# Issuing a transformer kernel's second batch from ScalarE before the first attention unit, and moving that batch's norm

## The chip, the core and the metric

The kernel runs on one core of a Trainium2 chip, as one launch. The metric is the device time in microseconds of one execution, taken as the median of several. Five engines work on their own instruction streams, each in its own order: PE (TensorE, matmuls), ACT (ScalarE), DVE (VectorE), POOL (GpSimd) and SP (SyncE, which only issues DMAs here). ACT and POOL can issue DMAs as well; such an issue stands in their stream like any other instruction. In the profile SPq and ACTq are these issues, PEld is PE's loading of weights. All arithmetic is in 32-bit floats. "Round" and "unit" below are words of this kernel.

## What is computed

Two transformer layers over x of shape (4, 512, 320), with a context of shape (4, 1601, 192). Each layer is:

```
h1 = layernorm(x) * n1_g + n1_b
x  = softmax((h1 q1)(h1 k1)^T / 4) (h1 v1) o1_w + o1_b + x        # 20 heads of 16
h2 = layernorm(x) * n2_g + n2_b
x  = softmax((h2 q2)(ctx k2)^T / 4) (ctx v2) o2_w + o2_b + x      # 1601 keys
h3 = layernorm(x) * n3_g + n3_b
a, g = split(h3 ff_w1 + ff_b1)
x  = (a * gelu(g)) ff_w2 + ff_b2 + x
```

## The kernel before

The work is cut into units: for each layer, self attention (4 batches by 5 groups of 4 heads), cross attention (the same 20), and one feed-forward unit per batch. A self-attention unit has 4 key chunks of 128. For every unit the kernel computes, ahead of the unit itself,

- the projections (`both`, line 786): two calls per unit, `proj` in the chains below. PE multiplies the normalised tokens hT by q1 and k1 (line 794), ACT brings the result out as `low` (line 810; for the first unit ACT makes `high`, line 805, and DVE `low`, line 806), and POOL splits it into a high and a low part (`split`, lines 714 and 715; not for the first unit).
- the moves (line 762): six DMAs that bring high and low parts of keys and queries into the places from which PE reads them. In the opening they go to SP and ACT in turn, high parts by SP and low parts by ACT.
- the values (`values`, line 926 on PE, copied by ACT at line 933): two parts by four chunks of tokens per batch, of 128 and of 192 columns.
- the row maxima (`max_pairs`): rounds of 8 matmuls into 4 PSUM banks (line 992), each bank reduced by DVE (line 1007). A self-attention unit has four rounds. `max_end` (lines 1057 to 1069) turns the maxima into rows `nrows`, by one DVE transpose and four small DMAs, in the opening by SP, ACT, POOL and SP.

The unit itself (`main`, line 1189) computes scores (line 1199), takes the exponential on ACT (line 1209), multiplies by the values (line 1225), and adds up on POOL (line 1245), with rounds of maxima of the next unit between. A batch's norm (`add_norm`) has, in the chain `norm`: four steps of statistics on DVE (lines 520, 521); two steps that find 1/sqrt by Newton's method (three DVE operations at lines 484 to 488, then line 490 and three times lines 497 to 500, on DVE while `start["on"]` holds and on POOL afterwards); four steps that normalise (line 537, DVE); three that transpose on PE and bring hT out (ACT, line 560; in the opening the middle one on DVE, line 555), each followed on POOL by adding a bias row `brow` to x (line 566).

In the steady state chains of such tasks are picked by due time and a credit of PE time, round by round (`steps`, `pick`, `pace`). Ahead of the first unit the order is written out by hand: the lines that the diff removes at its end. PSUM has 8 banks, and `bank` gives each new tile the bank that a table of assumed costs (`written`, `busy`) expects to be free first. Every instruction waits in its engine's order until what it needs is there, so a tile given a bank whose old content has not been read yet holds PE up.

Loads before the change, all by SP, in this order: x of batch 0 in four pieces of 160 KB (line 160), the norm's scales and shifts lng and lnb (three small DMAs each, line 198), q1, k1 and v1 in three pieces each (line 193), two bias rows brow broadcast to 128 partitions (line 201), x of batch 1 in four pieces. After them come the six moves of the first unit.

Of the kernel before, what the change touches and what calls it, by code (L numbers as in the profile page):

```python
# [9 lines left out]
F32 = mybir.dt.float32  # L10
# [14 lines left out]
NQ = N // P  # L25
# [41 lines left out]
def kernel(ctx: ExitStack, tc: tile.TileContext, x, context, ws, out):  # L67
# [16 lines left out]


    nc = tc.nc
    dma = nc.sync.dma_start

    const = ctx.enter_context(tc.tile_pool(name="const", bufs=1))
    wpool = ctx.enter_context(tc.tile_pool(name="weights", bufs=1))  # L90
# [36 lines left out]
    room = {"turn": 0, "first": 0}  # L127
# [27 lines left out]
    def load_x(b):  # L155

        src = x[b].rearrange("(c p) d -> p c d", p=P)

        def part(t):
            dma(out=xs[b][:, t], in_=src[:, t])  # L160
            loaded[b] = clock["round"] if t == NQ - 1 else 1 << 30

        return [lambda t=t: part(t) for t in range(NQ)]
# [24 lines left out]
    def now(fs):  # L188
        for f in fs:
            f()  # L190
# [9 lines left out]
    def load_row(t, v):  # L200
        dma(out=t, in_=v.rearrange("(o d) -> o d", o=1).to_broadcast([P, D]))

    def load_bias(l, i):
        if i > 2:
            l, i = l + 1, i - 3
        if l < L:
            load_row(brow[(3 * l + i) % 2], ws[l][("o1_b", "o2_b", "ff_b2")[i]])
# [8 lines left out]
    def load_self(l):  # L216
        return [lambda: load_norm(l, 0)] + [
            f for t, n in ((wq1, "q1"), (wk1, "k1"), (wv1, "v1")) for f in load_rows(t, ws[l][n], DK)
        ]
# [107 lines left out]
    units = []  # L327
# [35 lines left out]
    stage = [0] * B  # L363


    start = {"on": True}

# [52 lines left out]
    def run(chain):  # L422
        costs, _, ready, _, f = chains[chain].popleft()
        assert ready(), chain
        f()
        clock["credit"] -= sum(costs)
# [54 lines left out]
    def guess_root(var):  # L481

        a, h, y, z = (two.tile([P, NQ], F32, tag=f"root{i}", name=f"root{i}") for i in range(4))
        nc.vector.tensor_scalar(a, var, EPS, None, ALU.add)
        nc.vector.tensor_scalar(
            z.bitcast(I32), a.bitcast(I32), 1, None, ALU.logical_shift_right
        )
        nc.vector.tensor_scalar(y.bitcast(I32), z.bitcast(I32), -1, 0x5F3759DF, ALU.mult, ALU.add)
        eng = nc.vector if start["on"] else nc.gpsimd
        eng.tensor_scalar(h, a, -0.5, None, ALU.mult)  # L490
        return h, y, z

    def better_root(h, y, z):


        eng = nc.vector if start["on"] else nc.gpsimd
        eng.tensor_tensor(z, y, y, ALU.mult)
        eng.tensor_tensor(z, z, h, ALU.mult)
        eng.tensor_scalar(z, z, 1.5, None, ALU.add)
        eng.tensor_tensor(y, y, z, ALU.mult)  # L500
# [216 lines left out]
    def add_proj(u):  # L717
        chain = "early" if u.early else "proj"
# [3 lines left out]
        first = units[u.i - u.g]  # L722
# [29 lines left out]
        def move(of, pairs, may, gap=0):  # L752

            def f():
                pending[of] -= 1
                u.moving[of] = clock["round"]
                for to, src in pairs():
                    queue = nc.sync
                    if start["on"]:
                        queue = (nc.sync, nc.scalar)[room["first"] % 2]  # L760
                        room["first"] += 1
                    queue.dma_start(out=to.bitcast(F32), in_=src)
                u.open -= 1
                if not u.open:
                    u.when = -9 if start["on"] else clock["round"]

            pending[of] += 1
            u.moves[of].append((f, may, gap))
            u.moving[of] = clock["round"]
            if (u.i, of, u) not in movers:  # L770
                movers.append((u.i, of, u))
# [273 lines left out]
    def max_reduce(u):  # L1045
        if u.pm is not None:
            nc.vector.tensor_reduce(
                u.nm.rearrange("p (j t) -> p t j", t=NQ), u.pm, AX.X, ALU.max, negate=True
            )
            busy("dve", 0.25)  # L1050

    def max_end(u):

        parts = two.tile([P, SLOT], F32, tag="parts", name="parts")
        high, low = (parts.rearrange("p (j e t) -> p e j t", e=2, t=NQ)[:, e] for e in range(2))
        of = u.nm.rearrange("p (j t) -> p j t", t=NQ)
        nc.vector.tensor_copy(high.bitcast(F32R), of)
        nc.vector.tensor_tensor(low, of, high, ALU.subtract)
        turned = two.tile([P, SLOT], F32, tag="turned", name="turned")

        nc.vector.transpose(turned, parts)
        busy("dve", 0.6)
        slots = u.rows.bitcast(F32).rearrange("(g s) n -> s g n", s=DH)[0].rearrange("g (t r) -> g t r", t=NQ)

        def rows():
            for i in range(P // SLOT):
                part = slice(i * SLOT, (i + 1) * SLOT)
                queue = (nc.sync, nc.scalar, nc.gpsimd, nc.sync)[i] if start["on"] else nc.sync
                queue.dma_start(out=slots[:, :, part], in_=turned[part, :])

        if u.cross and u.before.cross:
            errands.appendleft((clock["round"] + 1, yes, rows))
        else:
            rows()
# [368 lines left out]
    def at_once(v):  # L1443
        chain = "early" if v.early else "proj"
        while not v.keyed:
            if not chains[chain][0][2]():
                for w in attn:
                    for todo in w.moves.values():
                        while todo and todo[0][1]():
                            todo.popleft()[0]()  # L1450
            run(chain)
        for todo in v.moves.values():
            while todo:
                assert todo[0][1]()
                todo.popleft()[0]()
# [60 lines left out]

    take_rooms(0)
    now(load_x(0))
    now(load_self(0))
    load_bias(0, 0)  # L1520
    load_bias(0, 1)
    now(load_x(1))

    add_norms(0)
    add_proj(units[0])
    warm(5)
    until(lambda: not chains["proj"], "proj")
    at_once(units[0])
    add_proj(units[1])
    add_values(units[0])  # L1530
    run("proj")
    run("proj")
    for _ in range(2 * NQ + 2):
        run("norm")
    at_once(units[1])
    add_proj(units[2])
    first = units[0]
    first.pairs = max_pairs(first)
    for chain in ("proj", "proj", "values", None):
        round_of(first.pairs[0].popleft() + first.pairs[1].popleft())  # L1540
        if chain:
            run(chain)

    at_once(units[2])
    run("values")
    max_reduce(first)
    max_end(first)
    loads.extend(load_x(2))
    for fs in (load_out(0, "o1_w"), load_x(3), load_cross(0)):
        loads.extend(fs)  # L1550
    second = units[1]
    second.pairs = max_pairs(second)
    for _ in range(2):
        round_of(second.pairs[0].popleft() + second.pairs[1].popleft())
        run("values")
        run("values")
    start["on"] = False
    clock["credit"] = 0.0

# [46 lines left out]
```

## Time and profile before

| | |
|---|---|
| median of 3 runs | 3083.38 us (3080.82 to 3083.61) |
| the profiled execution | 3081.84 us |
| its span, first to last instruction | 3080.1 us |
| TensorE clock granted, mean | 0.988 |
| busy: PE, DVE, ACT, POOL | 97%, 72%, 64%, 37% of the span |
| first matmul of the first unit's scores | 43.41 us into the span |

The times in the timeline are microseconds from the span's start: start, duration, engine, line, operation, what is written and read, how often, and in brackets how long the engine was idle before it and what ended that. Consecutive instructions of one kind are one row. DMA rows tell of the issue, not of the transfer. The view by stages gives for each stretch its length, then busy time and number of instructions of each engine, the granted clock, the busy share of the DMA engines and GB/s.

### The profile page before, as it was taken

To read this page: it belongs to the slowest core of one execution; us is meant where nothing else is said; L and a number is where in the kernel's file an instruction comes from. 1 tells how busy PE (TensorE), PEld (TensorE's weight loads), DVE (VectorE), ACT (ScalarE), POOL (GpSimd) and SP (SyncE) were. 2 spreads that over 40 slices of the span, in tenths; PEclk is the share of its full clock that TensorE was granted. 3 is DMA by queue.
4 is the path that set the end of the run, shared out by engine and by line. 5 is a ranking of instruction groups with operands and counts; after the bars stand their busy time and mean duration, and the time that the engine had idled before them with its cause. 6 is when DMAs were issued, how large, how long until landed. Compare 5 with 4: busy or idle time off the path is not lost.

```text
span 3080.1 us, 82562 instructions
## 1 busy us (share of the span) xinstructions
PE 2986.1 (97%) x34290; PEld 1615.6 (52%) x34290; DVE 2220.3 (72%) x4240; ACT 1962.2 (64%) x3909; POOL 1125.7 (37%) x1209
## 2 busy tenths in 40 slices
PE   8999999999999999999999999999999999999999
PEld 5555455555555555455555555555545555544555
DVE  6987888888888888422258888888888888784221
ACT  4776577877877878611137765778778778784110
POOL 3444234544544544301114442445444444431000
PEclk9999899999999999999999999999999999999999
DMA  4433222221221221300113331212121122102000
GB/s 104 127 85 98 53 63 57 62 59 35 62 59 34 62 54 27 83 6 0 31 45 106 84 81 51 61 50 47 43 55 42 43 59 47 44 16 80 9 13 13
DMA packets 188327, 165.62 MB, mean 54 GB/s; under 512 B 67748, under 2 KB 152880, under 8 KB 187952
## 3 DMA queue, kind: packets, MB, share of 16 engines
q1 hardware_dynamic: 187160, 159.15, 20.2%
q8 instruction: 270, 4.42, 0.6%
q10 hardware_dynamic: 760, 1.18, 0.1%
q14 instruction: 105, 0.86, 0.1%
q0 software_dynamic: 32, 0.00, 0.0%
HBM read 43.53 MB, written 28.90 MB: 24 GB/s over the span
## 4 chain that ended last, share of the span: by engine, by line
PE 75%; DVE 21%; ACT 1%; issue 1%; POOL 1%; SPq 1%; DMA 0%; ACTq 0%; DVEq 0%
PE av L1225 18%; PE st L1199 15%; DVE pm L1007 10%; PE fps L1328 9%; PE sps L992 8%; PE yps L1385 6%; DVE nmax L1007 4%; PE kps L860 3%; PE qkps L794 3%; PE ops L1127 3%; PE vps L945 3%; PE fps L1342 2%; PE vps L926 2%; PE qps L835 1%; PE sps L1019 1%; DVE oturn L1095 1%
## 5 line engine op out<-in xcount | busy, mean ns | idle before, releaser
L1209 ACT ACTIVATE pr<-st 128x512 f32<-128x512 f32 (+1 forms) x2720 | 1408.2, 604 | 318.1 <-PE st L1199 249.1
L1007 DVE TENSOR_REDUCE pm<-sps 128x1 f32<-128x512 f32 x1920 | 1183.7, 680 | 76.7 <-PE sps L992 67.5
L1245 POOL TENSOR_TENSOR o<-o,vo 128x512 f32<-128x512 f32 x576 | 739.5, 1284 | 1257.1 <-ACT vo L1244 1245.7
L992 PE MATMUL sps<-kT,q 32*128 32x512 f32 x4800 | 960.9, 443 | 29.7 <-DVE x L1134 11.3
L1199 PE MATMUL st<-q,kT 32*128 32x512 f32 (+1 forms) x5120 | 837.3, 427 | 8.8 <-DVE pm L1007 8.6
L1225 PE MATMUL av<-pr,vals 128*32 128x512 f32 (+1 forms) x5440 | 746.9, 614 | 33.3 <-DVE pm L1007 10.2
L1199 PEld LDWEIGHTS st<-q,kT 32*128 32x128 f32 (+1 forms) x5120 | 442.6, 181 | 409.9 <-ACT pr L1209 214.7
L1199 PE MATMUL st<-nrows,ones 32*128 32x512 f32 (+1 forms) x2720 | 565.2, 407 | 0.3 <-DMA nrows<-turned 0.3
L992 PEld LDWEIGHTS sps<-kT,q 32*128 32x128 f32 x4800 | 456.7, 186 | 137.8 <-DVE pm L1007 46.9
L1007 DVE TENSOR_REDUCE nmax<-sps 128x1 f32<-128x512 f32 x640 | 395.1, 681 | 74.7 <-PE sps L992 72.5
L1244 ACT COPY vo<-av 128x512 f32<-128x512 f32 x576 | 352.2, 612 | 51.3 <-PE av L1225 50.0
L1353 ACT ACTIVATE gl<-fps,b 128x512 f32<-128x512 f32 x80 | 54.7, 687 | 374.0 <-PE fps L1342 267.8
L1328 PE MATMUL fps<-hT,w 128*128 128x512 f32 x640 | 283.5, 596 | 0.0
L1225 PEld LDWEIGHTS av<-pr,vals 128*32 128x32 f32 (+1 forms) x5440 | 112.3, 108 | 296.8 <-DVE pm L1007 136.3
L1199 PEld LDWEIGHTS st<-nrows,ones 32*128 32x128 f32 (+1 forms) x2720 | 253.8, 181 | 17.3 <-issue 1.1
L1354 DVE SCALAR_TENSOR_TENSOR hid<-fps,b,gl 128x512 f32<-128x512 f32 x80 | 59.8, 750 | 238.6 <-ACT gl L1353 236.2
L1328 PEld LDWEIGHTS fps<-hT,w 128*128 128x128 f32 x640 | 119.4, 190 | 148.9 <-issue 146.7
L1385 PE MATMUL yps<-w,hid 128*128 128x320 f32 x640 | 175.7, 434 | 0.0
L1385 PEld LDWEIGHTS yps<-w,hid 128*128 128x128 f32 x640 | 120.7, 190 | 55.1 <-ACT gl L1353 4.5
L1127 PEld LDWEIGHTS ops<-wo,aT 112*32 112x32 f32 (+1 forms) x3072 | 97.2, 110 | 65.1 <-issue 43.8
L1127 PE MATMUL ops<-wo,aT 112*32 112x160 f32 (+1 forms) x3072 | 123.8, 300 | 3.9 <-DVE pm L1007 3.6
L1392 DVE TENSOR_TENSOR x<-yps,x 128x320 f32<-128x320 f32 x32 | 15.7, 492 | 153.4 <-PE yps L1385 153.4
(90 smaller groups left out, 2562.4 us busy)
## 6 DMA issues: line engine op xcount, KB each, us to landing
kT<-stages SPq DMA_DIRECT2D x160, 192.0 KB
oway<-o SPq DMA_DIRECT2D x80, 256.0 KB
q<-high SPq DMA_DIRECT2D x160, 64.0 KB
q<-low SPq DMA_DIRECT2D x160, 64.0 KB
kT<-high SPq DMA_DIRECT2D x60, 128.0 KB
q<-high SPq DMA_DIRECT2D x60, 128.0 KB
kT<-low SPq DMA_DIRECT2D x57, 128.0 KB
aT<-oway SPq DMA_DIRECT2D x32, 224.0 KB
```

Source lines behind the costliest of these rows:

```text
L794: nc.tensor.matmul(ps[:, :w], lhsT=wqk[:n, k, u.g].rearrange("p i d -> p (i d)"), rhs=first.hT[:n, k, at : at + w], start=(k == 0), stop=( ...
L860: nc.tensor.matmul(ps[i * GD : (i + 1) * GD, :w], lhsT=wk_q[rows, k, u.g * GD : (u.g + 1) * GD], rhs=first.kvT[rows, k, i * HALF : i * HAL ...
L992: nc.tensor.matmul(ps, lhsT=u.q[j * SLOT : (j + 1) * SLOT, e, t * P : (t + 1) * P], rhs=u.kT[j * SLOT : (j + 1) * SLOT, u.k0 + s * 512 : u ...
L1007: nc.vector.tensor_reduce(to[:, j : j + 1], ps, AX.X, ALU.max, negate=(ns == 1))
L1127: nc.tensor.matmul(ps[f : f + m, : D // 2], lhsT=aT[:n, k, t * P + f : t * P + f + m], rhs=wo[:n, k, cols], start=(k == 0), stop=(k == 2),)
L1199: nc.tensor.matmul(st[:r, :], lhsT=ones[rows, :r] if e == 2 else u.keys(rows, c), rhs=u.rows[rows, :] if e == 2 else u.q[rows, e, :], star ...
L1209: nc.scalar.activation(p[:r], st[:r], AF.Exp)
L1225: nc.tensor.matmul(ps[j * SLOT : (j + 1) * SLOT, :], lhsT=columns_of[:r, head : head + SLOT], rhs=pr.pop((c, j))[:r, :], start=True, stop= ...
L1244: nc.scalar.copy(vo, ps)
L1245: nc.gpsimd.tensor_tensor(u.o, u.o, vo, ALU.add)
L1328: nc.tensor.matmul(ps, lhsT=w1[:, k, i * FF + c * P : i * FF + (c + 1) * P], rhs=u.hT[:, k, :], start=ahead and k == 0, stop=not ahead and ...
L1385: nc.tensor.matmul(ps[:, :D], lhsT=hid[c][:, t * P : (t + 1) * P], rhs=w2[:, c, :], start=(c == 0), stop=(c == NHC - 1),)
```

## The change

Only the opening differs; nothing is computed differently. Loads: x of batch 1 is issued by ACT as its first instructions, beside SP's load of batch 0; SP then issues lng, lnb, q1 and k1, and ACT v1 and the two bias rows. In program order batch 1's x now stands before lng. The Newton steps of batch 1 go to POOL (`start["first"]` is off once the first unit's projections and moves are issued). Its statistics and Newton steps come before the second unit's projections, its four normalising steps only after the first unit's four rounds of maxima and `max_end`, ahead of two rounds of the second unit. Of the values, seven of eight steps instead of six run before the first unit. The rest is a renaming.

```diff
-    dma = nc.sync.dma_start
+    queue = [nc.sync]
+
+    def dma(**tensors):
+        queue[0].dma_start(**tensors)
+
+    def by(engine, fs):
+        queue[0] = engine
+        for f in fs:
+            f()
+        queue[0] = nc.sync
...
-    start = {"on": True}
+    start = {"on": True, "first": True}
...
-        eng = nc.vector if start["on"] else nc.gpsimd
+        eng = nc.vector if start["on"] and start["first"] else nc.gpsimd
         eng.tensor_scalar(h, a, -0.5, None, ALU.mult)
...
-        eng = nc.vector if start["on"] else nc.gpsimd
+        eng = nc.vector if start["on"] and start["first"] else nc.gpsimd
...
     take_rooms(0)
     now(load_x(0))
-    now(load_self(0))
-    load_bias(0, 0)
-    load_bias(0, 1)
-    now(load_x(1))
+    by(nc.scalar, load_x(1))
+    parts = load_self(0)
+    now(parts[:7])
+    by(nc.scalar, parts[7:] + [lambda i=i: load_bias(0, i) for i in range(2)])
 
     add_norms(0)
     add_proj(units[0])
     warm(5)
     until(lambda: not chains["proj"], "proj")
     at_once(units[0])
+    start["first"] = False
     add_proj(units[1])
     add_values(units[0])
-    run("proj")
-    run("proj")
-    for _ in range(2 * NQ + 2):
-        run("norm")
-    at_once(units[1])
-    add_proj(units[2])
-    first = units[0]
-    first.pairs = max_pairs(first)
-    for chain in ("proj", "proj", "values", None):
-        round_of(first.pairs[0].popleft() + first.pairs[1].popleft())
-        if chain:
-            run(chain)
-
-    at_once(units[2])
-    run("values")
-    max_reduce(first)
-    max_end(first)
+    first, second = units[:2]
+    first.pairs, second.pairs = max_pairs(first), max_pairs(second)
+    for what in "norm norm norm norm norm norm proj proj moves1 values max proj proj max values values max values max moves2 rows values norm norm norm norm max2 values max2 values".split():
+        if what == "max":
+            round_of(first.pairs[0].popleft() + first.pairs[1].popleft())
+        elif what == "max2":
+            round_of(second.pairs[0].popleft() + second.pairs[1].popleft())
+        elif what == "moves1":
+            at_once(units[1])
+            add_proj(units[2])
+        elif what == "moves2":
+            at_once(units[2])
+        elif what == "rows":
+            max_reduce(first)
+            max_end(first)
+        else:
+            run(what)
     loads.extend(load_x(2))
     for fs in (load_out(0, "o1_w"), load_x(3), load_cross(0)):
         loads.extend(fs)
-    second = units[1]
-    second.pairs = max_pairs(second)
-    for _ in range(2):
-        round_of(second.pairs[0].popleft() + second.pairs[1].popleft())
-        run("values")
-        run("values")
     start["on"] = False
     clock["credit"] = 0.0
```

More of the change, by code (lines that the diff above doesn't have):

```diff
@@ L757, in f @@
                 for to, src in pairs():
-                    queue = nc.sync
+                    way = nc.sync
                     if start["on"]:
-                        queue = (nc.sync, nc.scalar)[room["first"] % 2]
+                        way = (nc.sync, nc.scalar)[room["first"] % 2]
                         room["first"] += 1
-                    queue.dma_start(out=to.bitcast(F32), in_=src)
+                    way.dma_start(out=to.bitcast(F32), in_=src)
                 u.open -= 1
@@ L1067, in rows @@
                 part = slice(i * SLOT, (i + 1) * SLOT)
-                queue = (nc.sync, nc.scalar, nc.gpsimd, nc.sync)[i] if start["on"] else nc.sync
-                queue.dma_start(out=slots[:, :, part], in_=turned[part, :])
+                way = (nc.sync, nc.scalar, nc.gpsimd, nc.sync)[i] if start["on"] else nc.sync
+                way.dma_start(out=slots[:, :, part], in_=turned[part, :])
         if u.cross and u.before.cross:
```

## The prediction

> **What bounds the kernel now.** I read the page first, then the stages, then the chain of waits through the opening, then the timeline there. The page's first part and three rows of the view by stages:
>
> ```profile
> PE 2986.1 (97%) x34290; PEld 1615.6 (52%) x34290; DVE 2220.3 (72%) x4240; ACT 1962.2 (64%) x3909; POOL 1125.7 (37%) x1209
> ```
> ```profile
> 22.00:43.40 21.40, 18.82 (x204) 11.09 (x204) 19.47 (x46) 2.23 (x7) 3.81 (x4) 0.74 0.33 84
> 43.40:73.00 29.60, 29.13 (x272) 18.14 (x268) 17.40 (x33) 21.19 (x42) 12.81 (x13) 1.00 0.30 77
> ...
> 300.00:3080.00 2780.00, 2706.11 (x31026) 1452.97 (x31022) 1977.39 (x3731) 1770.42 (x3522) 1000.01 (x1053) 0.99 0.19 48
> ```
>
> PE bounds the whole. From 43.4 us, where the first unit begins, it is busy 29.13 of 29.60 us, while DVE has room. Before that DVE leads: 19.47 of 21.40 us. So the change can move the time by the shift of the first unit's start and by matmuls moved to where PE waits anyhow. The chain, from 12 to 44 us:
>
> ```profile
> 12.06 6.84 DMA x<-in_x_dram
> ...
> 25.68 1.51 DVE hn L537 x4
> ...
> 40.17 0.27 ACT vals L933
> ```
>
> It runs through batch 1's load, its norm on DVE, then maxima, with a copy on ACT near the end. The change attacks the first two.
>
> **The load, ahead of the first unit's norm.**
>
> ```profile
> 0.73 1.82 SPq L160 DMA_DIRECT2D x<-in_x_dram  x4
> ...
> 4.00 1.36 SPq L198 DMA_DIRECT2D lnb<-in_L_xattn_n_b_dram  x3
> ...
> 5.40 0.46 DVE L520 BATCH_NORM_STATS2 st<-x 128x6 f32<-128x320 f32 x1
> 5.41 2.04 SPq L193 DMA_DIRECT2D wqk<-in_L_xattn_q_dram  x3
> ...
> 6.07 1.28 ACT L560 ACT_TABLE_LOAD   x1 [6.07 <-DMA lnb<-in_L_xattn_n_b_dram]
> ...
> 7.50 1.97 SPq L193 DMA_DIRECT2D wqk<-in_L_xattn_k_dram  x3
> ...
> 11.11 0.91 SPq L201 DMA_DIRECT2D brow<-in_L_xattn_o_b_dram  x2
> 11.20 1.65 ACT L560 ACTIVATE hT<-hps,lnb,lng 112x512 f32<-112x512 f32 x2 [3.85 <-PE hps L551]
> ...
> 12.03 5.50 PE L794 MATMUL qkps<-hT,wqk 112*128 112x256 f32 x24
> ```
> ```profile
> SPq L762 <- DMA brow<-in_L_xattn_o_b_dram: 1.8, 1, 1.8
> ...
> SPq L762 <- DMA x<-in_x_dram: 1.3, 2, 0.8
> ```
> ```profile
> 1.50:5.00 3.50, 3.46 (x4) 1.51 (x5) 1.46 (x5) 0.00 (x0) 3.40 (x2) 1.00 0.69 188
> ```
>
> The waits of SP tell a rule of the program: the move that waits for brow is the 28th DMA and the first brow the 20th. Eight semaphores in turn fit this; I take it that each DMA waits until the one eight before it has landed. Now batch 1's x is 5th to 8th, and this bites: lnb's first (12th) waits for the fourth piece of batch 0, q's (15th to 17th) for batch 1's last pieces and lng, ACT's second brow (25th) for q's third piece.
>
> Batch 0's 655 KB took the stretch of the last row at 188 GB/s with the DMA engines 0.69 busy. With both batches at once the fourth piece, used at 5.40, lands between 5.4 (nothing shared) and 8.5 (1311 KB at 188 GB/s from 1.5); at 188/0.69 = 272 GB/s it would be 6.3 plus the receipt. I take 6.8. q then starts 5.41 - 4.00 = 1.41 later, at 8.2, and its third piece at 9.6. Landing takes 2.1 (lnb's first piece: issued at 4.00, released ACT at 6.07) to 3.2 us (k's third piece, issued at 8.8, was there for PE's run from 12.03); with 3.0 it is there at 12.6, ACT has issued the last brow at 13.05, and only then comes its table load of 1.28, which is cheap now because ACT idles at 6.07. hT begins at 14.35 instead of 11.20. **The first unit is late by 3.15 us**, with the bounds combined 0.8 to 5.0.
>
> The Trainium skill, "DMA: Bandwidth & Descriptors", section "Issuing engines are not separate DMA queues", speaks against this change: DMAs from several engines share the same 16 DMA engines, and a second issuer saves only issue time. By that rule the load of batch 1 takes from batch 0, as assumed here; if the second queue brought its own bandwidth, the delay would be 1.75 us (5.4 in place of 6.8). The 0.69 above leaves room for something between.
>
> **The first maxima.**
>
> ```profile
> 15.47 0.48 DVE L806 SCALAR_TENSOR_TENSOR low<-qkps,scales,high 128x256 f32<-128x256 f32 x1 [0.76 <-ACT high L805]
> 15.99 0.55 ACTq L762 DMA_DIRECT2D kT<-low  x1
> ...
> 17.94 3.30 POOL L566 TENSOR_TENSOR x<-x,brow 128x320 f32<-128x320 f32 x4 [11.53 <-DMA kT<-high]
> 18.46 1.58 ACTq L762 DMA_DIRECT2D q<-low  x2
> 18.92 0.49 DVE L520 BATCH_NORM_STATS2 st<-x 128x6 f32<-128x320 f32 x1 [2.96 <-DMA x<-in_x_dram]
> ...
> 21.20 0.61 POOL L714 CAST high<-low 128x512 fp32r<-128x512 f32 x1
> ...
> 21.51 0.32 DVE L484 TENSOR_SCALAR root<-mv 128x4 f32<-128x4 f32 x1
> ...
> 21.88 1.28 POOL L715 TENSOR_TENSOR low<-low,high 128x512 f32<-128x512 f32 x1
> ...
> 21.93 1.37 PE L992 MATMUL sps<-kT,q 32*128 32x512 f32 x8 [4.40 <-DMA q<-low]
> ...
> 22.06 1.13 DVE L488 TENSOR_SCALAR root<-root 128x4 int32<-128x4 int32 x1
> ...
> 23.19 0.47 ACTq L762 DMA_DIRECT2D kT<-low  x1
> ...
> 23.70 1.48 ACTq L762 DMA_DIRECT2D q<-low  x2
> ...
> 27.11 4.87 DVE L1007 TENSOR_REDUCE nmax<-sps 128x1 f32<-128x512 f32 x8
> ```
>
> DVE ends the first unit's low part at 15.95 + 3.15 = 19.1, then does batch 1's statistics (18.92 to 21.51: 2.6) and three operations of the root: 0.55 to 1.68, taken as 0.75, since the 1.13 of L488 stands beside POOL's subtraction, which is elsewhere now. It is free at 22.45. The moves no longer stand behind batch 1: ACT issues its three in 0.55 + 1.58, by 21.3, they land 1.9 later (20.04 to 21.93), and the first reduce comes 0.7 after that (below: matmuls at 40.49, reduce at 41.20), **at 23.9 instead of 27.11**. Here the change does what it says.
>
> **What is late next.** Three edits meet. The Newton steps now stand on POOL ahead of the second unit's split, ACT's three DMAs of the second unit's low parts wait for that split, and behind them on ACT stand the copy of the first value chunk and the third unit's projections.
>
> ```profile
> 101.18 0.20 POOL L497 TENSOR_TENSOR root<-root 128x4 f32<-128x4 f32 x1 [0.16 <-DVE root L488]
> ...
> 104.34 0.20 POOL L500 TENSOR_TENSOR root<-root,root 128x4 f32<-128x4 f32 x1
> ```
> ```profile
> 38.58 2.44 DVE L1007 TENSOR_REDUCE nmax<-sps 128x1 f32<-128x512 f32 x4
> 38.69 1.44 ACTq L1069 DMA_DIRECT2D nrows<-turned  x1
> ...
> 40.49 0.90 PE L992 MATMUL sps<-kT,q 32*128 32x512 f32 x7 [1.05 <-ACT vals L933]
> ...
> 41.20 2.48 DVE L1007 TENSOR_REDUCE nmax<-sps 128x1 f32<-128x512 f32 x4 [0.18 <-PE sps L992]
> ...
> 43.41 0.50 PE L1199 MATMUL st<-q,kT 32*128 32x512 f32 x2
> ...
> 62.02 1.16 PE L926 MATMUL vps<-wv,hT 112*32 112x192 f32 x24
> ```
>
> POOL: the first brow is issued behind the landing of q's second piece, at 11.9, and lands, with the 6.8 us of 11.11 to 17.94, at 18.7; the additions take 3.3, to 22.05; the twelve Newton operations run from 22.45 in 3.36 (101.18 to 104.54), to 25.8; the split 1.96, to 27.8. ACT: three issues of 0.47 + 1.48 and a gap, 1.99, to 29.8; the copy 0.27, to 30.1. That copy matters because the second round of maxima gets the copied bank: following `written` and `busy` by hand through the new order, the four banks expected free first are the second unit's second projection (12.16), the value chunk (12.87) and two of the first round (13.76, 14.36). PE stands there, as the row at 40.49 shows it waiting for such a copy, and **the second round is reduced at 30.8**, 1.3 later than before (27.11 + 2.44 = 29.55); 4.5 us of DVE's gain are idle time.
>
> Rounds two to four take 3 x 2.44, to 38.1, `max_end` 0.63 (before, 38.02 to 38.65), to 38.75, and now the four normalisings 1.51, to 40.25. Beside these ACT issues its nrows DMA behind `max_end` (1.44) and then copies the fifth value chunk, at 40.55; by the same table its bank (21.94 against 22.02 for the next) goes to the fifth round, reduced from 41.3. With 2.44, 0.18 and 2.48 the sixth ends at 46.4, against 41.20 + 2.48 = 43.68: the first unit starts 2.7 late. The value chunk moved ahead is worth 1.1 (62.02: 1.16, less the overlap with its neighbours), since PE waits for DVE there. **Sum: +2.7 - 1.1 = +1.6 us**, between -0.8 and +3.5 by the bounds above. The low granted clock (0.74 in the row of 22 to 43.4 us) adds nothing to this sum: PE waits there either way. The loads of v1 and the renaming are free: PE needs v1 after the moves.
>
> On the profiled execution's own 3081.84 us (span 3080.1 and 1.7 around it) that is 3083.4. The median shown is 3083.38, 1.5 above that execution, so the forecast for a median is **3085.0 us**. I count 0.2%, 6.2 us, as what a measurement of this kernel can tell from no change.
>
> **The rivals.** B: the copy is not waited for (another bank, or POOL done early). Then DVE runs from 23.9 without a gap: six rounds 14.7, 0.63, 1.51 and 0.2, to 40.9; 2.8 and 1.1 are won: 3079.5. For it: only one place in the order of banks. Against: POOL and ACT work in order, and ACT's copies stand behind DMA issues at 38.69 already. C: the same, and the first unit isn't late, because batch 1's load fits beside batch 0's and the waits by eights fall on landed DMAs: 3.15 more, 3076.4. Against: even with every lower bound (5.4 + 1.41 + 1.36 + 2.1 + 0.45 + 1.28) hT begins at 12.0, not 11.20. D, the slower side: brow's landing. POOL's additions stand ahead of the Newton steps; from 0.4 us later than assumed each microsecond delays the second round by one. The 6.8 us of 11.11 to 17.94 were the slowest transfer of the opening; beside q and k on the other queue, and with its broadcast source, twice that is 6.4 more: 3091.4. E: the one value chunk less shifts the picks of later rounds. PE idles 2780 - 2706.1 = 73.9 us after 300 us; a tenth dealt otherwise is 7.4 us either way: 3077.6 or 3092.4. That the change doesn't do what it says (DVE's time saved, ACT's queue put in its place) is the forecast itself.
>
> **Chances.** Forecast 0.50, with its own range 3081 to 3089 (bounds, and 1.5 for the spread of runs); B 0.17; C 0.12; D 0.10; E 0.11, a little more of it slower. Faster by over 0.2% (below 3077.2): C and 0.05 of E, 0.17. Slower (above 3089.5): D and 0.06 of E, 0.16. Within: forecast and B, 0.67. The range 3076.4 to 3090.0 leaves out half of C, most of D and of E's upper part, under 0.2.
>
> **What would show it.** Right: hT at about 14.3, with the table load just before it; the first reduce near 24, then a gap of DVE of some 4 to 5 us that ends with a copy of values behind ACT's DMAs; the Newton steps on POOL from 22.5; the first scores near 46. Wrong: hT before 13; the second round straight after the first; PE's idle time past 300 us off by more than 4 us from 73.9, which would make the opening the smaller part of the answer.

## The result and the profile after

The changed kernel takes **3084.04 us** (median of 22 executions, 3081.71 to 3089.61). The kernel before, run 22 times beside it, takes 3078.28 us (3073.1 to 3086.15). The ratio is 1.0018 with a 95% interval of 1.0011 to 1.0024: slower by 5.8 us, between about 3.4 and 7.4. The profiled execution took 3085.45 us with a span of 3083.7 us; that of before had 3081.84 and 3080.1.

Lines of the changed kernel stand 10 higher than those of before in most places (L794 is now L804, L1007 is L1017, L1199 is L1209), and all loads carry L90, the new helper. The page's first part after:

```profile
PE 2987.0 (97%) x34290; PEld 1617.6 (52%) x34290; DVE 2217.3 (72%) x4227; ACT 1963.4 (64%) x3909; POOL 1130.0 (37%) x1222
```

Thirteen small operations went from DVE to POOL, no more; over the whole span nothing shows. The view by stages of the changed kernel (length, busy time and count of PE, PEld, DVE, ACT, POOL, then the granted clock, the DMA share and GB/s):

```profile
12.00:22.00 10.00, 8.95 (x32) 7.24 (x32) 4.06 (x7) 2.50 (x4) 3.43 (x4) 0.66 0.38 78
22.00:44.00 22.00, 15.56 (x177) 10.13 (x176) 14.09 (x33) 3.08 (x9) 7.27 (x18) 0.84 0.45 109
44.00:57.30 13.30, 13.30 (x90) 7.75 (x87) 7.55 (x12) 3.29 (x7) 0.00 (x0) 0.50 0.05 14
...
300.00:3080.00 2780.00, 2708.49 (x31141) 1455.68 (x31134) 1982.26 (x3740) 1777.97 (x3536) 1005.54 (x1057) 0.99 0.19 48
```

The same stretches of before:

```profile
12.00:22.00 10.00, 5.60 (x29) 4.44 (x28) 4.29 (x13) 2.56 (x5) 3.98 (x6) 0.87 0.77 203
22.00:44.00 22.00, 19.43 (x216) 11.64 (x218) 19.75 (x46) 2.55 (x8) 3.81 (x4) 0.75 0.32 82
44.00:57.30 13.30, 13.03 (x108) 8.16 (x102) 9.47 (x18) 8.77 (x17) 4.00 (x5) 1.00 0.01 2
```

Two things are to be seen. Between 22 and 44 us DVE, which led there, is busy 14.09 instead of 19.75 us: it waits. And from 44 to 57.3 us PE is busy throughout at half its clock (0.50), where it had the full one; ACT, which takes the exponentials of the first unit, does 3.29 us of work instead of 8.77.

What the opening costs in all is read at one mark: the first projection of context keys, a PE operation of the steady state. The view by tile gives its first start, for before and then for after:

```profile
L860 PE MATMUL kps<-ctxT,w x3840: 347/348/631, 247.3 to 2679.9; 32*64 32x224 f32 x192
```
```profile
L870 PE MATMUL kps<-ctxT,w x3840: 347/348/576, 256.9 to 2682.9; 32*64 32x224 f32 x192
```

The opening costs **9.6 us** in this pair (a second pair, below, gives 9.5). The order of PE's work after the opening is the same in both traces. With neighbouring matmuls into the same tile taken as one group, and scores and maxima as one kind, there are some 1860 groups, and apart from a few missing records, such as two traces of one kernel also show, only the first 28 differ. So the 9.6 us come from the opening. They are more than the medians differ by; that remainder is taken up at the end.

The opening itself, from the timeline of the changed kernel:

```profile
3.64 2.41 SPq L90 DMA_DIRECT2D lng<-in_L_xattn_n_g_dram  x3
3.83 3.76 ACTq L90 DMA_DIRECT2D wv<-in_L_xattn_v_dram  x3
...
7.53 1.47 SPq L90 DMA_DIRECT2D lnb<-in_L_xattn_n_b_dram  x3
7.54 0.49 DVE L530 BATCH_NORM_STATS2 st<-x 128x6 f32<-128x320 f32 x1 [1.08 <-DMA x<-in_x_dram]
7.90 0.84 ACTq L90 DMA_DIRECT2D brow<-in_L_xattn_o_b_dram  x2
...
9.58 1.28 ACT L570 ACT_TABLE_LOAD   x1 [9.58 <-DMA lnb<-in_L_xattn_n_b_dram]
11.28 2.60 DVE L547 TENSOR_SCALAR hn<-x,mv,root 128x320 f32<-128x320 f32 x4
...
11.88 3.55 POOL L576 TENSOR_TENSOR x<-x,brow 128x320 f32<-128x320 f32 x4 [5.46 <-DMA lnb<-in_L_xattn_n_b_dram]
...
14.44 0.78 ACT L570 ACTIVATE hT<-hps,lnb,lng 112x512 f32<-112x512 f32 x1 [3.57 <-PE hps L561]
...
15.90 7.25 PE L804 MATMUL qkps<-hT,wqk 112*128 112x256 f32 x24
...
27.21 5.49 PE L804 MATMUL qkps<-hT,wqk 112*128 112x256 f32 x12
27.24 2.49 DVE L1017 TENSOR_REDUCE nmax<-sps 128x1 f32<-128x512 f32 x4 [2.64 <-PE sps L1002]
...
28.00 0.61 POOL L724 CAST high<-low 128x512 fp32r<-128x512 f32 x1
...
29.99 0.47 ACTq L772 DMA_DIRECT2D kT<-low  x1
30.50 1.45 ACTq L772 DMA_DIRECT2D q<-low  x2
31.99 0.27 ACT L943 COPY vals<-vps 128x128 f32<-128x128 f32 x1 [7.62 <-issue]
...
32.63 1.07 PE L1002 MATMUL sps<-kT,q 32*128 32x512 f32 x8
...
33.72 2.49 DVE L1017 TENSOR_REDUCE nmax<-sps 128x1 f32<-128x512 f32 x4 [4.00 <-PE sps L1002]
```

The fourth piece of batch 0 is used at 7.54 instead of 5.40, hT begins at 14.44 instead of 11.20, and the first maxima are reduced at 27.24, no earlier than before (27.11). Then DVE waits 4.00 us for the second round. One of that round's banks holds the first value chunk, which ACT copies only at 31.99, behind its three DMAs; these wait for POOL's split at 28.00. But PE isn't free earlier either. It works on the second unit's projections from 27.21 to 32.70, at half clock (0.51 granted over 27.0 to 33.5 us): twelve matmuls take 5.49 us, where e3 to e5 below have 2.86 at the full clock. The copy is done at 32.26, and PE goes on to the second round at 32.63 without a gap. So here two causes end at nearly the same time; the experiments tell them apart. The timeline further on:

```profile
41.69 1.45 ACTq L1079 DMA_DIRECT2D nrows<-turned  x1
...
43.18 0.32 ACT L943 COPY vals<-vps 128x192 f32<-128x192 f32 x1 [6.23 <-DVE hn L547]
43.55 1.18 PE L1002 MATMUL sps<-kT,q 32*128 32x512 f32 x5 [4.40 <-ACT vals L943]
44.45 2.48 DVE L1017 TENSOR_REDUCE nmax<-sps 128x1 f32<-128x512 f32 x4 [1.39 <-PE sps L1002]
44.66 2.15 PE L936 MATMUL vps<-wv,hT 112*32 112x192 f32 x24
...
48.40 2.15 PE L936 MATMUL vps<-wv,hT 112*32 112x192 f32 x24
50.47 0.79 PE L1209 MATMUL st<-q,kT 32*128 32x512 f32 x2
```

PE stands idle for 4.40 us until ACT, behind its nrows DMA, has copied the fifth value chunk. When PE starts again at 43.55 it has half its clock: 24 matmuls of values take 2.15 us (1.16 at full clock, in the row at 62.02 of before), and the first scores come at 50.47 instead of 43.41.

### The profile page after: what moved, and what is told of

Read it like the earlier page. It is cut to its first block, busy times and chain, and to the rows that moved or that the text cites. A ratio compares the mean times of both kernels' runs of the same rounds, so it can differ in the third digit from the quotient of the medians.

```text
span 3083.7 us, 82559 instructions
## 1 busy us (share of the span) xinstructions
PE 2987.0 (97%) x34290; PEld 1617.6 (52%) x34290; DVE 2217.3 (72%) x4227; ACT 1963.4 (64%) x3909; POOL 1130.0 (37%) x1222
## 4 chain that ended last, share of the span: by engine, by line
PE 75%; DVE 22%; ACT 1%; issue 1%; POOL 1%; DMA 1%; SPq 0%; ACTq 0%; DVEq 0%
PE av L1235 18%; PE st L1209 15%; DVE pm L1017 10%; PE fps L1338 9%; PE sps L1002 7%; PE yps L1395 6%; DVE nmax L1017 5%; PE qkps L804 4%; PE kps L870 3%; PE ops L1137 3%; PE vps L955 3%; PE fps L1352 2%; PE vps L936 2%; PE qps L845 1%; PE sps L1029 1%; DVE oturn L1105 1%
## 5 line engine op out<-in xcount | busy, mean ns | idle before, releaser
L1017 DVE TENSOR_REDUCE pm<-sps 128x1 f32<-128x512 f32 x1920 | 1182.9, 680 | 74.1 <-PE sps L1002 65.5
L1209 PE MATMUL st<-q,kT 32*128 32x512 f32 (+1 forms) x5120 | 835.9, 426 | 9.3 <-DVE pm L1017 9.0
L1209 PEld LDWEIGHTS st<-q,kT 32*128 32x128 f32 (+1 forms) x5120 | 441.1, 181 | 411.5 <-ACT pr L1219 215.4
L1209 PE MATMUL st<-nrows,ones 32*128 32x512 f32 (+1 forms) x2720 | 564.1, 406 | 0.0
L1017 DVE TENSOR_REDUCE nmax<-sps 128x1 f32<-128x512 f32 x640 | 395.0, 681 | 82.3 <-PE sps L1002 77.8
L1209 PEld LDWEIGHTS st<-nrows,ones 32*128 32x128 f32 (+1 forms) x2720 | 252.6, 180 | 16.3
```

What stands on the lines that cost most here:

```text
L1017: nc.vector.tensor_reduce(to[:, j : j + 1], ps, AX.X, ALU.max, negate=(ns == 1))
L1209: nc.tensor.matmul(st[:r, :], lhsT=ones[rows, :r] if e == 2 else u.keys(rows, c), rhs=u.rows[rows, :] if e == 2 else u.q[rows, e, :], star ...
```

## The experiments

Two theories stood against each other after this reading. The first: the new order puts waits behind ACT's DMAs into the opening, and the second of them costs twice, since the idle PE loses its clock just where the PE-bound unit starts. The rival: the loads do it, through the later norm of the first unit, and the order only passes the delay on. Each run below gives the median and the record's ratio to the kernel before, which was run beside it, with its 95% interval. The ratio isn't the quotient of the two medians and differs from it by up to 0.0007.

**e1_old_loads**: the changed kernel with the loads as before.

```diff
-    by(nc.scalar, load_x(1))
-    parts = load_self(0)
-    now(parts[:7])
-    by(nc.scalar, parts[7:] + [lambda i=i: load_bias(0, i) for i in range(2)])
+    now(load_self(0))
+    load_bias(0, 0)
+    load_bias(0, 1)
+    now(load_x(1))
```

> The changed kernel, with the loads as before (all by SP, batch 1's x last). The mark is the start of the first projection of context keys: 247.3 us before, 256.9 after. Theory: the loads make the first unit's low part late by 5.6 us (21.57 against 15.95), and ACT's DMA issues behind POOL's split make the second round late. With the old loads the low part ends near 16, but batch 1's x lands near 18.9, so the Newton steps on POOL start near 22.2 and the second round near 30.5 instead of 33.7: the mark at 253.7, the time 3 us under the changed kernel. Rival 1, the loads cost nothing and only the order of the engines' work does: the mark stays at 256 to 257. Rival 2, the loads are the whole loss: the mark at 247 to 248.

Measured: 3082.82 us, ratio to before 1.0010 (0.9997 to 1.0022). The first reduce is at 22.51, the second round at 29.24 after a wait of 4.25, the fifth at 39.97, the first scores at 46.03, the mark at 250.2. The mark was expected at 253.7. With an early norm DVE's waits of the new order are still there. In the second round PE again comes late by its half clock: the projections take 5.41 us, until 27.86, and PE then stands only 0.42 us for the copy.

**e2_only_loads**: the kernel before with the new loads (the reverse of that diff).

> The kernel before, with the new loads alone. Theory: the low part ends near 21.6, statistics, Newton steps and normalising of batch 1 on DVE follow, the first reduce comes at 28.7 instead of 27.1, and the mark (247.3 before) at about 249, the time 1 to 2 us over before. Rival 1, loads cost nothing: 247.3. Rival 2, loads are the whole loss: 256 to 257, 6 us or more over before.

Measured: 3076.82 us, ratio 0.9991 (0.9981 to 1.0000). First reduce 29.17, first scores 45.46, mark 249.4. In the profile the loads alone delay the opening by 2, as expected; the median does not show it.

**e3_newton_dve**: the changed kernel with batch 1's Newton steps on DVE, by leaving out one line.

```diff
-    start["first"] = False
```

> The changed kernel, with batch 1's Newton steps on DVE again. Theory: DVE waits for the moves until 27.2 anyhow, so 2.4 us of Newton steps cost it nothing, while POOL's split starts at 24.4 instead of 28.0 and ACT is free at 28.4 instead of 32.0: the second round near 30, the mark at 253.3, the time 3 us under the changed kernel. Rival 1, that POOL is not in the way (PE or the bank is): the second round stays at 33.7, the mark at 257. Rival 3, that DVE needed the relief: the first reduce at 29 or later, the mark at 258 or more.

Measured: 3084.35 us, ratio 1.0016 (1.0006 to 1.0025). Its timeline has the four rounds of the first unit in one row, then the fifth:

```profile
26.61 9.65 DVE L1017 TENSOR_REDUCE nmax<-sps 128x1 f32<-128x512 f32 x16
39.71 2.48 DVE L1017 TENSOR_REDUCE nmax<-sps 128x1 f32<-128x512 f32 x4 [1.39 <-PE sps L1002]
```

The wait of 4.00 us is gone: with the Newton steps off POOL, the split, ACT's DMAs and the copy (26.77) are in time. But the projections also have the full clock here (2.86 us from 25.36), so this run alone doesn't say which of the two did it. The wait before the fifth round stays (PE idle 4.40 us, half clock after it); scores at 45.77, mark at 251.3. The 3 us that were expected in the time don't show in the ratio.

**e4_moves_sp**: the second unit's moves all by SP, so that ACT's copy stands behind no DMA.

```diff
-                        way = (nc.sync, nc.scalar)[room["first"] % 2]
+                        way = nc.sync if u.i == 1 else (nc.sync, nc.scalar)[room["first"] % 2]
```

> The changed kernel, with the second unit's six moves all issued by SP, so that ACT's copies don't stand behind them. Theory: the first value chunk is copied at about 24.4, the second round follows the first without a gap, at 29.7 instead of 33.7, the mark at 252.9, the time 4 us under the changed kernel. The fifth round still waits for ACT's nrows DMA. Rival 1, the bank isn't what holds PE: the second round stays at 33.7. Rival 2, the clock: PE's half speed from 26.5 to 33.4 sets the second round, which then comes at 31 to 32.

Measured: 3084.75 us, ratio 1.0020 (1.0010 to 1.0030). Its timeline:

```profile
22.31 0.27 ACT L943 COPY vals<-vps 128x128 f32<-128x128 f32 x1
...
28.40 7.26 DVE L1017 TENSOR_REDUCE nmax<-sps 128x1 f32<-128x512 f32 x12 [1.01 <-PE sps L1002]
...
38.22 1.22 PE L1002 MATMUL sps<-kT,q 32*128 32x512 f32 x5 [4.40 <-ACT vals L943]
```

The copy comes at 22.31, and the wait of the second round shrinks to 1.01; the projections again have the full clock (2.86 us from 24.84). The second wait is untouched. Scores 45.18, mark 249.3 (252.9 was expected). The 4 us expected in the time don't show in the ratio. The profiled execution took 3074.33 us, the other nine 3082.02 to 3087.94, so its mark may not be theirs.

**e5_pe_filled**: the changed kernel with `warm(5)`, ten matmuls of no use in the trace, before the fifth round, where PE would stand idle. (`warm` also takes a PSUM bank and enters its cost in the table by which `bank` chooses.)

```diff
-... rows values norm norm norm norm max2 values max2 values".split():
+... rows values norm norm norm norm fill max2 values max2 values".split():
...
+        elif what == "fill":
+            warm(5)
```

> The changed kernel, with five more dummy matmuls (the identity on a filled tile, as at the start; their output is read by nothing) ahead of the fifth round of maxima, where PE idles 4.4 us behind the copy of the fifth value chunk and its clock is then granted at half for 10 to 14 us, in the first unit. Theory: the loss after 43 us is the half clock; with PE kept busy the clock stays whole, the values and scores of 43.5 to 57.3 run at full speed, and the mark (first projection of context keys, 256.9) comes at 252 to 254, the time 3 us under the changed kernel. Rival: the wait alone is the loss, half clock or not, since DVE's maxima set the pace: the mark stays at 256 to 257 or goes up by what the dummies delay, the time the same or 1 us more.

Measured: 3080.47 us, ratio 1.0009 (1.0000 to 1.0019). Its timeline:

```profile
30.56 1.22 PE L1002 MATMUL sps<-kT,q 32*128 32x512 f32 x7 [2.09 <-ACT vals L943]
...
31.42 2.48 DVE L1017 TENSOR_REDUCE nmax<-sps 128x1 f32<-128x512 f32 x4 [3.67 <-PE sps L1002]
...
38.81 4.56 PE L408 MATMUL wps<-fill,ident 128*128 128x512 f32 x10
...
42.77 0.32 ACT L943 COPY vals<-vps 128x192 f32<-128x192 f32 x1 [5.33 <-DVE hn L547]
...
43.97 1.18 PE L936 MATMUL vps<-wv,hT 112*32 112x192 f32 x24
44.07 4.28 DVE L1017 TENSOR_REDUCE nmax<-sps 128x1 f32<-128x512 f32 x7 [1.44 <-PE sps L1002]
...
45.75 1.19 PE L936 MATMUL vps<-wv,hT 112*32 112x192 f32 x24
46.86 0.50 PE L1209 MATMUL st<-q,kT 32*128 32x512 f32 x2
```

and its stages:

```profile
39.00:43.50 4.50, 4.50 (x14) 1.83 (x17) 3.53 (x10) 0.32 (x1) 0.85 (x1) 1.00 0.31 67
43.50:57.30 13.80, 13.60 (x137) 7.96 (x134) 11.34 (x19) 6.41 (x13) 1.87 (x2) 1.00 0.04 13
```

The fifth round is reduced at 44.07, nearly when it was (44.45). But the clock stays full: values take 1.18 instead of 2.15, and the scores follow the fifth round by 2.79 us instead of 6.02. The mark is 251.3 instead of 256.9. So work that computes nothing kept PE's clock and brought the unit on earlier; in the ratios, 1.0009 against 1.0018, the intervals overlap. The first two rows bear on the second round: in this execution the projections before it had the full clock (2.86 us from 25.19), and PE then stood 2.09 us for ACT's copy, with DVE waiting 3.67. So the copy alone makes nearly all of that wait too.

**e6_no_gaps**: the second unit's moves by SP, and the order "... max moves2 values rows max2 norm norm norm norm values max2 values", which puts the fifth value chunk ahead of `rows` and the fifth round ahead of the norm.

> The changed kernel, with the second unit's moves all by SP, the fifth value chunk ahead of the rows' DMAs, and the four normalising steps between the fifth and the sixth round instead of ahead of both. Theory: no wait of PE behind ACT's DMA issues is left; first scores at about 42 to 43 instead of 45.2 (the moves by SP alone) and 50.5 (changed), the clock not at half in the first unit, the mark at 246 to 247, the time 5 to 8 us under the changed kernel and as fast as before or faster. Rival: the time after the opening is what differs (the banks that the assumed costs give out from there on): the mark falls, the time stays near 3084.

Measured: 3081.56 us, ratio 1.0009 (0.9999 to 1.0018). Reduces at 24.8, 28.3, 30.7, 33.1, 36.15 and 39.94, scores at 39.92 (42 to 43 were expected), mark at 248.3 (246 to 247). Of the 5 to 8 us expected in the time, the ratio shows 2.8, with overlapping intervals. One wait is left: 2.00 us of PE (36.12 to 38.12) for the copy of the sixth chunk behind the nrows DMA, and half clock from 39.8 to 50.0 us after it.

**e7_before_again** and **e8_after_again**: both kernels again, one profile each.

> The kernel before, once more, for a second profile of its opening. If the clock's windows fall otherwise, the mark (247.3) moves; theory: by less than 2 us, since the half clock of its opening (19.5 to 33.1) lies where DVE is waited for. A rival by which the first profile of before was a lucky one has it at 250 or more.

> The changed kernel, once more, for a second profile of its opening: the two long gaps (second round about 4 us after the first has ended, fifth round behind a copy of values) must be there again; the mark, 256.9 in the first, may be 2 to 5 us less if the clock is not halved at 12.9 and 26.5.

Measured: before 3077.38 us, scores at 43.90, mark at 247.9; after 3084.23 us, scores at 51.73, mark at 257.3, and half clock again from 43.3 us on. The 9.6 us of the opening repeat as 9.5 (257.33 - 247.85).

**e9_late_x1**: the order of before; ACT issues v1, the bias rows and then batch 1's x, which stands behind q and k in program order.

```diff
+    parts = load_self(0)
+    now(parts[:7])
+    by(nc.scalar, parts[7:] + [lambda i=i: load_bias(0, i) for i in range(2)] + load_x(1))
```

> The kernel before, with v1, the bias rows and batch 1's x issued by ACT, but in program order after q1 and k1, so that batch 1's x is not ahead of the first unit's loads. Theory: batch 0's fourth piece is used at about 5.5 again (7.5 in the changed kernel), the first unit's low part ends at 16 to 17 (15.95 before, 21.6 changed), its moves don't wait for batch 1, the first reduce follows DVE's norm of batch 1 at 23 to 25 instead of 27.1, and the mark (first projection of context keys: 247.3 and 247.8 before) comes at 244 to 246; the time 2 us under before. Rival, a second queue slows the first loads whatever its order (bytes, not order): low part at 19 or later, mark at 248 or more.

Measured: 3076.39 us, ratio 1.0001 (0.9990 to 1.0011). Expectation and measurement part: the low part of the first unit ends at 20.28, not 16 to 17, and the mark is 248.8. Batch 0's fourth piece is used at 6.47, between before (5.40) and the changed kernel (7.54), the four normalisings take 2.60 us again, and the projections take 7.02 us, about half of them at half clock. Low part and mark are where the rival had them, but the slow normalising and the half clock have a part in that, not only the bytes.

**e10_no_gaps_late_x1**: e6 with the loads of e9.

> The kernel without ACT's gaps (second unit's moves by SP, fifth value chunk ahead of the rows, normalising between rounds five and six), with the loads of the run e9. Theory: both losses gone; low part at 16 to 17, first reduce at 21 to 22 (24.8 without the late x), first scores at 36 to 38 (39.9), the mark at 244 to 246, the time 2 to 4 us under before. Rival: with batch 1's x late, statistics wait for it and nothing is won: mark at 248.

Measured: 3076.47 us, ratio 0.9999 (0.9989 to 1.0009); first reduce at 24.5 (21 to 22 were expected), scores at 39.59 (36 to 38), mark at 246.5 (244 to 246).

**e11_bias_late**: the changed kernel with the two bias rows issued by SP behind k1, to test what makes the normalising 2.60 us long.

```diff
-    by(nc.scalar, parts[7:] + [lambda i=i: load_bias(0, i) for i in range(2)])
+    by(nc.scalar, parts[7:])
+    load_bias(0, 0)
+    load_bias(0, 1)
```

> The changed kernel, with the two bias rows issued by SP after k1 instead of by ACT early. Theory: in the changed kernel batch 0's normalising on DVE takes 2.60 us instead of 1.52 because POOL's four additions of the bias rows (11.9 to 15.4) run beside it; with the rows late those additions come after it, normalising takes 1.5 again, and the first unit's low part is earlier by about 1 us (20.5 where the clock falls as in the changed kernel). The two long waits stay, the mark falls by 1 us at most, the time within 2 us of the changed kernel. Rival: the slow normalising comes from the transfers landing beside it; then it stays at 2.6.

Measured: 3082.30 us, ratio 1.0003 (0.9993 to 1.0013). Its timeline:

```profile
10.28 1.51 DVE L547 TENSOR_SCALAR hn<-x,mv,root 128x320 f32<-128x320 f32 x4
...
12.35 0.78 ACT L570 ACTIVATE hT<-hps,lnb,lng 112x512 f32<-112x512 f32 x1 [2.36 <-PE hps L561]
...
16.52 3.32 POOL L576 TENSOR_TENSOR x<-x,brow 128x320 f32<-128x320 f32 x4 [10.11 <-DMA brow<-in_L_xattn_o_b_dram]
...
28.99 1.23 PE L1002 MATMUL sps<-kT,q 32*128 32x512 f32 x7 [2.20 <-ACT vals L943]
```

With POOL's additions at 16.52 the normalising has its 1.51 us back. The rival, transfers landing beside it, falls: over these 1.51 us the DMA engines moved 180 GB/s at a share of 0.79. The changed kernel's own trace agrees: its first normalising, alone, takes 0.45 us, and its fourth, beside the additions, 0.98. hT begins at 12.35, 2.1 earlier than in the changed kernel; 1.0 of this is an earlier start of the normalising (10.28 instead of 11.28), since the fourth piece of batch 0 came earlier here. First reduce 23.56, scores 48.22, mark 253.5, a fall of 3.4 where 1 at most was expected. The waits of the order remain: DVE waits 3.80 us for the second round, with PE idle for 2.20 until the copy, and PE stands 2.42 us before the fifth.

**e12_old_loads_no_gaps**: e6 with the loads of before.

> The kernel without ACT's gaps (second unit's moves by SP, fifth value chunk ahead of the rows, normalising between rounds five and six), with all loads by SP in the old order. Theory: low part at 16, first reduce at 22.5 as with the old loads, second round without a gap near 25.5, first scores at 37 to 38, the mark at 244 to 245 (247.3 and 247.8 before), the time 2 to 3 us under before. Rival: batch 1's late x moves the statistics and with them POOL's split, so that the fifth round waits for the second unit's moves: mark at 248.

Measured: 3078.39 us, ratio 0.9993 (0.9984 to 1.0003). First reduce 23.35, second round 28.69, scores 40.28, mark 247.3 (244 to 245 were expected). DVE still waits 2.85 us for the second round, though the copy is done at 20.9: PE is busy with the projections, 4.71 us in part at half clock. 2.00 us of PE waiting for the sixth chunk's copy remain, with a granted clock of 0.69 from 39 to 43.5 us and 0.85 after it, so scores 3.1 earlier than before end in a mark that is no earlier.

Side by side, the ratios to before:

| order | old loads | new loads |
|---|---|---|
| before's | 1 | 0.9991 (0.9981 to 1.0000) |
| the change's | 1.0010 (0.9997 to 1.0022) | 1.0018 (1.0011 to 1.0024) |
| e6's | 0.9993 (0.9984 to 1.0003) | 1.0009 (0.9999 to 1.0018) |

**The new order is what costs.** With the same new loads, before's order and the change's stand at 0.9991 and 1.0018, with intervals apart: 0.0027 of 3080, or 8 us. With the old loads the step is 0.0010, and its interval just holds no change. The loads alone are no loss in the median, against the rival. Beside an order that reaches the unit sooner they may be one (0.9993 against 1.0009, intervals that just overlap). No version beats before clearly; those without the long waits (e6, e10, e12) have 1 in their intervals. Which part of the new order costs how much the ratios don't show; that rests on the traces.

## Why the prediction was right or wrong

The forecast was 3085.0 us and the sign a small loss; measured were 3084.04 and, against before, +5.8 where the sum had +1.6. The forecast stood on a median for before that was 5 us above the one measured beside the changed kernel, and the two errors met: that the time came within 1 us is luck. The mechanisms held in part.

**The load of batch 1.** Right in kind: the fourth piece was used at 7.54 (forecast 6.8), lng and lnb waited for landed pieces, q was issued at 9.04 (8.2), hT began at 14.44 (14.35). The Trainium skill's rule in "DMA: Bandwidth & Descriptors", section "Issuing engines are not separate DMA queues", has DMAs of all issuers on the same engines, with only issue time to be saved by a second one. The 7.54 agrees with the sharing. But the two queues together moved 277 GB/s from 1.5 to 5.0 us, at a DMA share of 0.89, where the one had moved 188 at 0.69: the room that the forecast saw in the 0.69 was there. Whether more than issue time was saved no run here shows. And the way to 14.35 was wrong. ACT's second bias row did not wait for q's third piece: ACT issued both at 7.90, the table load came at 9.58 and not at 13.05. What filled the gap was a later start of the normalising (11.28 instead of 9.27) and its 2.60 us, which e11 shows to come of POOL's additions beside it; the early bias rows put them there. Two errors cancelled: the 14.35 is luck too.

**The first unit late by 3.15 us.** This is the first mis-sized term: 5.6. The low part ended at 21.57, not 19.1. The projections started 1.46 after hT (0.83 before), and at a granted clock of 0.66 the 24 matmuls took 7.25 us instead of 5.50: 3.24 + 0.63 + 1.75 = 5.62. The first reduce so came at 27.24, not 23.9, and the gain that this step promised was gone.

**The second round behind POOL and ACT.** Right in size: the wait was 4.00 us (forecast 4.5). The chain through POOL, ACT's DMAs and the copy is there as forecast, and in e5 and e11, with the full clock, it alone ends the wait (3.67 and 3.80 us, PE idle 2.09 and 2.20). But in both profiles of the changed kernel PE came last: its projections, at half clock, took 5.49 us, until 32.70 in the first, when the copy was done. The forecast had no term for that. Either cause alone made most of the wait: the copy in e5 and e11, the projections in e12 (2.85). In e3 and e4 both were gone.

**The fifth round behind the nrows DMA.** Right as a wait: the copy came 1.5 us after `max_end`, as reckoned. Its time, 44.45 against 41.3, is late by what the steps before had lost.

**"The low granted clock adds nothing to this sum: PE waits there either way."** This is the step that failed. It was nearly true of before, where half clock lay between 19.5 and 33.1 us and the full one was back when the unit began. There DVE, which led, waited 1.13 us for a PE that was busy at half clock:

```profile
33.11 4.88 DVE L1007 TENSOR_REDUCE nmax<-sps 128x1 f32<-128x512 f32 x8 [1.13 <-PE sps L992]
```

In the changed kernel half clock cost in three places: 1.75 us in the first unit's projections, part of the wait for the second round, and the first unit itself. There the 4.40 us of waiting ahead of the fifth round put half clock over 43.6 to 57.3 us, where PE is the bound: the scores shift by 7.06, and the mark by 9.6. e5 shows the price: with the fifth round at the same time (44.07 against 44.45) and PE kept busy through the wait, the scores come 3.6 and the mark 5.6 us earlier. The ratio falls by 0.0009, 2.8 us, with intervals that overlap: the traces show the mechanism, the medians only point the same way. On the clock, the Trainium skill's "TensorE: Matmul & The Clock Gate" (part 1, "The HAM clock gate") has half rate after at least one idle window of about 3.4 us and the full rate after at least one busy one as long. The first half agrees with the 4.40 us here, though in e6 and e12 a gap of 2.00 us in PE's work was followed by half clock too. The second gives no 13.7 us: PE was busy for 13.75 of the 13.80 us from 43.5 on and had half its clock for four times the 3.4.

**The value chunk moved (-1.1).** In the traces it can't be told apart from the clock.

**The rivals.** B (DVE without a gap) falls by the 4.00 us, and C (no late unit) by the 14.44. D falls too: brow was early, not late. E: PE's idle time between 300 and 3080 us is 71.5, against 73.9 before, within the 4 us named, and its order is the same; so the opening is the larger part.

**What stays open.** The opening costs 9.6 and 9.5 us in two pairs of profiles, the medians differ by 5.8 (3.4 to 7.4). From the mark to the end the profiles have 2832.7 and 2827.7 us for before, 2826.7 and 2825.1 for after, and 2822.7 to 2833.0 over the experiments: a spread as large as what is missing. Much of this spread goes with the half clock that an execution happens to get behind the mark: the traces' clock records show 62.3 us of it in the first profile of before, 34.9 in that of after and 27.0 in e4, and over the 14 profiles the time behind the mark grows by 0.26 us for each microsecond of it (correlation 0.83). So one profile against another tells little about the whole time. The executions list their mean granted clock, and the time goes with it (before, in one session: 3071.08 us at 0.993, 3084.84 at 0.987). A fit over some 230 of them, with one slope and a constant for each kernel, gives 1.7 us for each 0.001, and at equal clock after is 3.4 to 3.5 us over before (standard error 0.4), so some 2 of the 5.8 us stand with a lower mean clock. That isn't chance alone, since the mean counts the opening too: 27.3 us of half clock in after's profile against 13.7 in before's lower it by 0.002. Why the rest of the 9.6 isn't seen is not settled. Nor is why e3 and e4, whose profiled openings are 5.6 and 7.6 us shorter than after's, have medians like after's: only one execution of each was profiled, and e4's was its fastest. e2 and e4 reach the mark at 249.4 and 249.3, and their medians, taken in one session, are 7.9 us apart. So the mark of one profile doesn't give a kernel's median, and how much of the 5.8 us the waits and the half clock make is not shown.

## What to carry to other kernels

Before work or DMA issues go to another in-order engine, list what stands behind them there; here it was a copy that freed a PSUM bank, and PE stood 4.40 us for it. That gap, just ahead of a TensorE-bound stage, was paid twice, as the gap and as 13.7 us of half clock in the stage. Half clock can cost earlier too, where another engine leads: ask in each stage whether PE at half speed (here 5.49 us instead of 2.86 for the projections) would still be in time. When a load comes earlier, ask which work it sets free, and beside what that work will then run. And where two causes end a wait at nearly the same time, an experiment that happens to remove both doesn't say which it was; look at what the engine was doing up to its end.

## What was not expected of the hardware

- Four normalisings of 128x320 on DVE took 2.60 us beside POOL's additions of the same size, and 1.51 without them (e11), while DMAs ran at 180 GB/s. The additions themselves took 3.55 and 3.32.
- Half clock came in the traces in stretches of about 3.4, 6.8, 10.2 and 13.7 us. It outlasted the gap: 13.7 us in the changed kernel after 4.40 us of idling, with PE busy throughout. In e6 and e12 a wait of 2.00 us was followed by 10.2 and 6.8 us of it.
- With the same loads the half clock near 13 us lasted 6.8 us in both profiles of the changed kernel and 3.4 in e3, e4 and e5, and the first reduce came at 24.9 in e4 and 25.3 in e5 instead of 27.2 (in e3 DVE's Newton steps hold it until 26.6). What decides this no run here shows.
